# A three-layer graph network on one core: 28 of 98 receiver blocks summed from rows fetched by edge

## The chip, the core and the metric

The kernel runs on one core of one Trainium2 chip. The time is device microseconds from the start to the end of the launch, as the median of repeated runs. The core's engines work side by side, each through its own queue in order: TensorE (PE in the profile, with its weight loads shown as PEld), VectorE (DVE), ScalarE (ACT), GpSimd (POOL) and SyncE (SP, which here only issues transfers). Transfers run on 16 DMA engines.

## What is computed

There are 12,500 nodes with 64 values each, and 212,500 edges sorted by their receiving node (100,000 drawn pairs in both directions, and a loop for each node). Three mean-aggregating graph convolutions are followed by one network over edge attributes:

```
def _sage_conv(x, src, dst, Wl, Wr, b, n_nodes):
    msgs = x[src]
    summed = jax.ops.segment_sum(msgs, dst, num_segments=n_nodes)
    cnt = jax.ops.segment_sum(jnp.ones(src.shape[0], x.dtype), dst, num_segments=n_nodes)
    agg = summed / jnp.maximum(cnt, 1.0)[:, None]
    return agg @ Wl + x @ Wr + b
...
h = jnp.maximum(_layernorm(x, axis=-1), 0.0)
x = x + L0(h)        # three _sage_conv, relu after the first two
h = jnp.maximum(_layernorm(x, axis=-1), 0.0)
# L1: mean of the edge attributes by receiver, next to h, through 128->64->64->64
x = x + L1(h, edge_attr_64)
```

The segment sum is the work: for each receiver the rows of its senders are added, 17 edges per node on average.

## The kernel before

**Blocks and the matrix.** Nodes are cut into 98 blocks of 128. The kernel turns the edge list into a dense matrix of counts, senders by receivers, in 8-bit floats (a count in units of 1/64), and multiplies by it. One receiver block has 98 x 128 sender rows and 128 columns.

**Building it.** `index(j)` (L335) prepares four receiver blocks: one DVE pass over all tile heads (L340), three gathers on POOL (`ends`, `to`, `of`, all recorded on L330), some 30 small DVE instructions, and a transpose, which give for each edge its column number `col`, its low sender bits `lo` and a `weight`. `build` (L429) then takes a block in 26 steps, two at a time (`pair`, L434): per step DVE writes two one-hot tiles, `c` (128x245, L439) and `h` (128x128, L443), PE multiplies them (L447), and ACT writes two results as 16-bit words into the matrix tile `m` (L450). Two neighbouring blocks share one `m`, which SP stores to DRAM (`mat`, L466).

**Layer 0** (L482 to L509) walks over 49 pairs of blocks. While pair hp is multiplied, pair hp+1 is built. Node rows are held in SBUF as `parts`, each value split into three 16-bit parts. `dense` (L229) multiplies in two passes of 98 matmuls: the wide pass (L234) takes two parts of the rows as 128 weights, the narrow pass (L243) the third part as 64 weights, where even and odd sender blocks use the two halves of the array. In layer 0 the columns of one matmul are the 256 of a pair.

**Layers 1 and 2** (L547 to L699) read `mat` back through tiles `t` (L559, seven per group) and walk over 25 groups of four blocks, 512 columns per matmul (the last group has two blocks). `conv` (L251) adds the receiver's own rows (`turn`, L260) and multiplies by the weights (`mix`, L269 and L273); `relu_parts` (L217) writes the next layer's rows.

**Edges** are summed beside layer 2: for every block, `edge_sum` (L598) gathers 19 edges per partition (`raw`, L602) and their receivers (`eto`, L606), splits the values into three parts (ACT L612 and L614, POOL L613 and L615), writes 19 one-hots on DVE (`own`, L627) and adds with 19 matmuls (L631). `second` (L647) is the edge network.

**What sets the order.** PE's order is written by hand (`manual_schedule`): `woven` (L287) runs the dense matmuls and slips in the other pieces ("fills") at given fractions of a group. On the other engines the tile framework orders instructions and places the waits.

Of the kernel before, what the change touches and what calls it, by code (L numbers as in the profile page):

```python
# [9 lines left out]
F32 = mybir.dt.float32  # L10
I32 = mybir.dt.int32
BF16 = mybir.dt.bfloat16
U16 = mybir.dt.uint16
FP8 = mybir.dt.float8e3
# [23 lines left out]
EK = 19  # L38

# [21 lines left out]
def in_order(  # L61
# [23 lines left out]

    nc = tc.nc
# [4 lines left out]
    CW = HP * WD  # L91
    NG = -(-NB // 4)
    assert EP - sz.e >= EK and CW <= 256
# [23 lines left out]
    iota_l = const.tile([P, P], BF16, name="iota_l")  # L117
    pid = iota(const, "pid", 1, 1, per_partition=1)
# [5 lines left out]
    node0 = const.tile([P, NG], F32, name="node0")  # L124
    mask4 = const.tile([P, 4], F32, name="mask4")
# [60 lines left out]
    parts = [const.tile([P, NB, 3 * D], BF16, name=f"parts{i}") for i in range(2)]  # L186
    begins = const.tile([P, NG], F32, name="begins")
    cnt = const.tile([P, NG * 4], F32, name="cnt")
    inv = const.tile([P, NG * 4], F32, name="inv")
    twins = const.tile([P, NG, 4], F32, name="twins")  # L190
    nc.vector.memset(twins, 0.0)
    hts = [const.tile([D + 1, 4, P], F32, name=f"ht{i}") for i in range(2)]
    for t in hts:
        nc.gpsimd.memset(t[D : D + 1], 1.0)
    mat = [dram.tile([P, HP, 2 * P], U16, name=f"mat{i}") for i in range(HP)]

    ps_d = ctx.enter_context(tc.tile_pool(name="ps_dense", bufs=1, space=PSUM))
    ps_c = ctx.enter_context(tc.tile_pool(name="ps_conv", bufs=1, space=PSUM))
    conv_p = ctx.enter_context(tc.tile_pool(name="conv", bufs=2))
# [17 lines left out]
    def relu_parts(pool, o, to, bufs=None):  # L217

        n = o.shape[1]
        nc.scalar.activation(to[:, :, :D], o, AF.Relu)  # L220
        r = pool.tile([P, n, D], F32, name="rest", bufs=bufs)
        nc.vector.scalar_tensor_tensor(
            r, o, 0.0, to[:, :, :D], op0=ALU.max, op1=ALU.subtract
        )
        nc.scalar.copy(to[:, :, D : 2 * D], r)
        nc.vector.tensor_tensor(to[:, :, 2 * D :], r, to[:, :, D : 2 * D], op=ALU.subtract)


    def dense(rows, at, n):  # L229


        p1 = ps_d.tile([P, 4 * P], F32, name="p1")[:, :n]
        for i in range(NB):
            nc.tensor.matmul(  # L234
                p1, rows[:, i, : 2 * D], at(i), start=i == 0, stop=i == NB - 1
            )
            yield
        e1 = conv_p.tile([P, 4 * P], F32, name="e1", bufs=1)[:, :n]
        nc.scalar.copy(e1, p1)
        p2 = ps_d.tile([P, 4 * P], F32, name="p2")[:, :n]  # L240
        for i in range(NB):
            half = slice(D * (i % 2), D * (i % 2) + D)
            nc.tensor.matmul(  # L243
                p2[half], rows[:, i, 2 * D :], at(i), start=i < 2, stop=i >= NB - 2
            )
            yield
        agg = conv_p.tile([P, 4 * P], F32, name="agg")[:, :n]
        nc.vector.tensor_tensor(agg, e1, p2, op=ALU.add)  # L248
        return agg

    def conv(layer, rows, agg, j0, n):  # L251

        ht = hts[conv.turn]
        conv.turn ^= 1

        def turn():
            pt = ps_c.tile([D, 4, P], F32, name="pt")
            for k in range(n):
                for i in range(3):
                    nc.tensor.matmul(  # L260
                        pt[:, k, :], rows[:, j0 + k, D * i : D * i + D], identb,
                        start=i == 0, stop=i == 2,
                    )
            nc.scalar.copy(ht[:D, :n, :], pt[:, :n, :])

        def mix():
            po = ps_c.tile([P, 2, 4, D], F32, name="po")
            for k in range(n):
                nc.tensor.matmul(  # L269
                    po[:, 0, k, :], agg[:, k * P : (k + 1) * P], wl2[:, layer, :],  # L270
# [3 lines left out]
                    po[:, 1, k, :], ht[:, k, :], wr1[:, layer, :], start=True, stop=True  # L274
                )
            o = conv_p.tile([P, 4, D], F32, name="o")[:, :n, :]
            nc.vector.tensor_tensor(  # L277
                o, po[:, 0, :n, :], inv[:, j0 : j0 + n, None].to_broadcast([P, n, D]), op=ALU.mult
            )
            nc.vector.tensor_tensor(o, o, po[:, 1, :n, :], op=ALU.add)  # L280
            return o

        return turn, mix

    conv.turn = 0

    def woven(main, fills):  # L287

        fills = sorted(fills, key=lambda f: f[0])
        i = 0  # L290
        try:
            while True:
                while fills and fills[0][0] * 2 * NB <= i:
                    fills.pop(0)[1]()
                next(main)
                i += 1
        except StopIteration as e:
            for _, f in fills:
                f()
            return e.value  # L300


    with ExitStack() as s:
        idx = s.enter_context(tc.tile_pool(name="idx", bufs=2))
        ps_b = s.enter_context(tc.tile_pool(name="ps_build", bufs=3, space=PSUM))
        ps_i = s.enter_context(tc.tile_pool(name="ps_idx", bufs=1, space=PSUM))
        hot = s.enter_context(tc.tile_pool(name="hot", bufs=6))
        ln = s.enter_context(tc.tile_pool(name="ln", bufs=1))
        heads = s.enter_context(tc.tile_pool(name="heads", bufs=1)).tile([P, T], F32, name="heads")
        with tc.tile_pool(name="row", bufs=1) as r:  # L310
# [7 lines left out]
            for c in range(0, T, 512):  # L318
                n = min(512, T - c)
                ph = ps_b.tile([P, 512], F32, name="pb")  # L320
# [4 lines left out]
        mats = s.enter_context(tc.tile_pool(name="mats", bufs=3))  # L325
# [934 lines left out]
```

## Time and profile before

| what | value |
|---|---|
| median of 3 runs | 3513.1 us (3511.75 to 3513.64) |
| the profiled execution's own time | 3514.05 us |
| its span (first to last instruction) | 3512.3 us |
| granted TensorE clock | 0.992 |
| PE / DVE / ACT / POOL busy | 3350.0 / 2111.3 / 1196.0 / 750.7 us |
| HBM read and written | 389.97 and 160.56 MB |

A row of the profile's groups gives line, engine, operation, output<-inputs, the tile's shape, the count, then busy time in us and the mean duration of one in ns, then the idle time before the group and who ended it. Durations of neighbouring instructions on one engine can overlap, so their starts tell how fast they follow each other. PE matmuls are pipelined: the mean of one is a latency, and the busy time of a group divided by its count is nearer to its pace. A chain of waits lists start, length and what ran.

### The profile page before, as it was taken

How to read it: one execution, taken by the hardware profiler on the slowest of the kernel's cores; microseconds unless marked ns; L12 is line 12 of the kernel's file. 1: busy time of each engine (PE TensorE's matmuls, PEld its weight loads, DVE VectorE, ACT ScalarE, POOL GpSimd, SP SyncE). 2: the span in 40 equal slices, each digit the busy share in tenths (PEclk: the TensorE clock that was granted, in tenths of full speed). 3: DMA queues.
4: the chain of work that ended last, by engine and by line, in shares of the span. 5: the costliest groups of instructions: out<-in, count | busy, mean ns of one | idle time of the engine just before them, and what ended most of it. 6: DMA issues, size and time to landing. Idle time of an engine off the chain costs nothing.

```text
span 3512.3 us, 69396 instructions
## 1 busy us (share of the span) xinstructions
PE 3350.0 (95%) x26430; PEld 2019.0 (57%) x26430; DVE 2111.3 (60%) x9072; ACT 1196.0 (34%) x2101; POOL 750.7 (21%) x482
## 2 busy tenths in 40 slices
PE   1899999999999999999999999979999999999998
PEld 0566777777777777555454545544555555555555
DVE  8999999999999999300000000035556555555554
ACT  4555555555555555100000000022322322322232
POOL 1000000000000000000000000055555565555562
PEclk9999999999999999999999999989999999999999
DMA  2222222332223223645454545455455555555551
GB/s 45 115 116 118 115 116 115 137 129 115 115 120 146 115 111 134 233 155 220 155 212 165 202 176 191 170 218 181 176 182 211 204 206 181 176 183 211 204 193 53
DMA packets 168554, 555.12 MB, mean 158 GB/s; under 512 B 57793, under 2 KB 60386, under 8 KB 161938
## 3 DMA queue, kind: packets, MB, share of 16 engines
q1 hardware_dynamic: 133232, 478.53, 35.7%
q0 software_dynamic: 19648, 66.90, 5.6%
q10 hardware_dynamic: 15330, 5.16, 0.6%
q8 instruction: 208, 3.41, 0.4%
q14 instruction: 136, 1.11, 0.1%
HBM read 389.97 MB, written 160.56 MB: 157 GB/s over the span
## 4 chain that ended last, share of the span: by engine, by line
PE 84%; DVE 10%; issue 4%; DMA 1%; ACT 1%; POOL 0%; ACTq 0%; SPq 0%; DVEq 0%; POOLq 0%
PE p L234 40%; PE p L243 24%; PE pb L447 8%; PE pe L631 5%; DVE h L443 2%; DVE c L439 2%; PE po L273 2%; PE po L269 2%; PE pt L260 2%; DVE own L627 2%; PE ph L666 1%; PE mo L674 1%; DVE lower L340 0%; DVE junk L385 0%; PE mt L659 0%
## 5 line engine op out<-in xcount | busy, mean ns | idle before, releaser
L234 PEld LDWEIGHTS <-parts 128*128 128x128 bf16 x9702 | 937.2, 99 | 584.7 <-issue 46.2
L234 PE MATMUL p<-t,parts 128*128 128x512 fp8e3 (+1 forms) x4900 | 1106.7, 376 | 4.6 <-DMA t<-mat 4.6
L450 ACT CAST m<-pb 128x490 uint16<-128x490 f32 (+1 forms) x1274 | 717.4, 563 | 537.3 <-PE pb L447 534.4
L627 DVE TENSOR_SCALAR own<-iota_l,eplace 128x128 bf16<-128x128 bf16 x1862 | 548.2, 353 | 401.8 <-PE pe L631 401.4
L443 DVE TENSOR_SCALAR h<-iota_l,lo,weight 128x128 bf16<-128x128 bf16 x2548 | 779.8, 306 | 0.0
L439 DVE TENSOR_SCALAR c<-iota_c,col 128x245 bf16<-128x245 bf16 x2548 | 716.5, 281 | 10.9 <-PE pb L447 5.5
L243 PEld LDWEIGHTS <-parts 128*64 128x64 bf16 x9702 | 494.1, 109 | 387.8 <-issue 185.1
L234 PE MATMUL p<-m,parts 128*128 128x256 fp8e3 x4802 | 652.3, 273 | 0.6 <-ACT m L450 0.6
L243 PE MATMUL p<-t,parts 128*64 128x512 fp8e3 (+1 forms) x4900 | 584.4, 378 | 0.0
L447 PE MATMUL pb<-c,h 128*128 128x245 bf16 x2548 | 499.0, 274 | 52.4 <-DVE h L443 35.0
L248 DVE TENSOR_TENSOR agg<-e,p 128x256 f32<-128x256 f32 (+1 forms) x99 | 54.4, 549 | 603.2 <-PE p L243 600.3
L243 PE MATMUL p<-m,parts 128*64 128x256 fp8e3 x4802 | 409.3, 281 | 0.0
L602 POOL DMA_INDIRECT raw<-in_edge_dram,mine x98 | 93.7, 956 | 1124.9 <-DMA t<-mat 1098.6
L447 PEld LDWEIGHTS <-h 128*128 128x128 bf16 x2548 | 205.6, 98 | 204.0 <-DVE h L443 148.9
L613 POOL TENSOR_TENSOR erest<-raw,cut 128x1216 f32<-128x1216 f32 x98 | 244.2, 2492 | 202.2 <-issue 198.1
L631 PE MATMUL pe<-cut,own 128*128 128x192 bf16 x1862 | 227.0, 248 | 34.9 <-DVE own L627 17.5
L631 PEld LDWEIGHTS <-own 128*128 128x128 bf16 x1862 | 151.3, 98 | 166.4 <-issue 58.6
L615 POOL TENSOR_TENSOR cut<-erest,cut 128x1216 bf16<-128x1216 f32 x98 | 244.6, 2496 | 11.2 <-ACT cut L614 2.6
L612 ACT CAST cut<-raw 128x1216 bf16<-128x1216 f32 x98 | 118.1, 1205 | 275.6 <-PE pe L631 266.0
L277 DVE TENSOR_TENSOR o<-po,inv 128x128 f32<-128x128 f32 (+1 forms) x99 | 35.1, 354 | 271.8 <-PE po L273 271.6
L614 ACT CAST cut<-erest 128x1216 bf16<-128x1216 f32 x98 | 118.1, 1205 | 225.6 <-POOL erest L613 225.6
L330 POOL DMA_INDIRECT to<-in_dst_dram,at_i x25 | 23.6, 946 | 709.6 <-DVE at_i L358 595.8
(143 smaller groups left out, 1666.8 us busy)
## 6 DMA issues: line engine op xcount, KB each, us to landing
t<-mat SPq DMA_DIRECT2D x686, 448.0 KB, 6.1
mat<-m SPq DMA_DIRECT2D x49, 3136.0 KB, 10.0
xb<-in_x_dram SPq DMA_DIRECT2D x14, 224.0 KB, 2.7
xr<-in_x_dram ACTq DMA_DIRECT2D x24, 128.0 KB, 2.2
out_dram<-o SPq DMA_DIRECT2D x24, 128.0 KB, 2.0
raw<-in_edge_dram,mine POOLq DMA_INDIRECT x98, 5.4
eto<-in_dst_dram,mine POOLq DMA_INDIRECT x98, 3.7
here<-in_dst_dram ACTq DMA_DIRECT2D x4, 208.0 KB, 5.5
```

The source lines that it names most:

```text
L234: nc.tensor.matmul(p1, rows[:, i, : 2 * D], at(i), start=i == 0, stop=i == NB - 1)
L243: nc.tensor.matmul(p2[half], rows[:, i, 2 * D :], at(i), start=i < 2, stop=i >= NB - 2)
L439: nc.vector.tensor_scalar(c, iota_c, col[:, w : w + 1], None, op0=ALU.is_equal)
L443: nc.vector.tensor_scalar(h, iota_l, lo[:, w : w + 1], weight[:, w : w + 1], op0=ALU.is_equal, op1=ALU.mult,)
L447: nc.tensor.matmul(pb[:, i, :CW], h, c, start=True, stop=True)
L450: nc.scalar.copy(m[:, :, o : o + 2 * k].rearrange("p h (w d) -> p h w d", d=k), pb[:, :, :CW].rearrange("p w (h d) -> p h w d", d=WD)[:, : ...
L612: nc.scalar.copy(cut[:, :, :D], raw)
L613: nc.gpsimd.tensor_tensor(rest, raw, cut[:, :, :D], op=ALU.subtract)
L614: nc.scalar.copy(cut[:, :, D : 2 * D], rest)
L615: nc.gpsimd.tensor_tensor(cut[:, :, 2 * D :], rest, cut[:, :, D : 2 * D], op=ALU.subtract)
L627: nc.vector.tensor_scalar(o, iota_l, place[:, k : k + 1], 1.0 / UNIT, op0=ALU.is_equal, op1=ALU.mult,)
L631: nc.tensor.matmul(state["p"], o, cut[:, k, :], start=k == 0, stop=k == EK - 1)
```

## The change

Of the 98 receiver blocks, the first 28 (`GB`) no longer have a matrix. Their sums are made in every layer from the senders' rows themselves: rows are kept in DRAM (`h_d`, one copy per layer, 384 bytes a row), and 19 indirect transfers per block, each of 128 rows, bring them into a tile `got` in two halves (10 and 9). DVE writes the one-hots of a half in one instruction, and 19 matmuls of 192 columns add them up. The index lists `rows_of` and `place` for this are made in layer 0 from the edge list (`lists`).

The other 70 blocks keep the dense way, in 18 groups (17 of four blocks and one of two), in layer 0 too, where the matmuls now have 512 columns instead of 256. The group of two comes first in layer 0. Building writes the one-hots in batches of 6 or 8 steps, as two-tensor instructions on 16-bit values instead of instructions with a scalar per step; `h` takes a compare and a multiply. The one-hot buffers hold two batches, and PSUM's `pb` two tiles instead of three.

Rows of layer 0 and 1 leave through DRAM: layer 1 loads its rows again (`rows1`), layer 2 has them in SBUF (`rows2`) and in DRAM. The pieces between matmuls are placed by `Weave`: by the count of wide matmuls (`wide`), or at a place of the narrow pass (`narrow`). A fetched block comes every 61 wide matmuls. In layer 2 the edge sums lie at wide places only, ordered by need; their splitting subtractions moved from POOL to DVE, and their one-hots are batched. The checks at L512 to L544 moved into layer 1's loop.

```diff
+GB = 28
+H1 = 10
...
+    dense_groups = [(j, min(4, NB - j)) for j in range(GB, NB, 4)]
...
+    def onehot(pool, codes, k0, k1):
+        n = k1 - k0
+        t = pool.tile([P, H1, P], BF16, name="own")
+        nc.vector.tensor_tensor(
+            t[:, :n].rearrange("p k (c t) -> p k c t", t=2),
+            iota_l.rearrange("p (c t) -> p c t", t=2)[:, None].to_broadcast([P, n, D, 2]),
+            codes[:, k0:k1, None, :].to_broadcast([P, n, D, 2]),
+            op=ALU.is_equal,
+        )
+        return t
+
+    HALVES = ((0, H1), (H1, EK))
...
+        def fetch(self, i):
...
+            b, (k0, k1) = i // 2, HALVES[i % 2]
+            t = self.got.tile([P, H1, 3 * D], BF16, name="got")
+            for k in range(k0, k1):
+                nc.gpsimd.indirect_dma_start(
+                    out=t[:, k - k0, :], out_offset=None, in_=h_rows[self.l],
+                    in_offset=bass.IndirectOffsetOnAxis(ap=rows_of[:, b, k : k + 1], axis=0),
+                )
...
+        def use(self, b):
...
+            for h, (k0, k1) in enumerate(HALVES):
+                i = 2 * b + h
+                self.mark(i + 1)
+                o, t = self.owned.pop(i), self.fetched.pop(i)
+                for k in range(k0, k1):
+                    nc.tensor.matmul(
+                        self.pg[:, b % 2, :], o[:, k - k0, :], t[:, k - k0, :],
+                        start=k == 0, stop=k == EK - 1,
+                    )
+                self.fetch(i + self.bufs)
...
+            cuts = [(0, 8), (8, 14), (14, 20), (20, QW)]
...
+            def hots(i):
...
+                nc.vector.tensor_tensor(
+                    split(tc_), pairs(iota_c, CW), own(col, CW), op=ALU.is_equal
+                )
+                th = hot.tile([P, 8, P], BF16, name="h")
+                nc.vector.tensor_tensor(split(th), pairs(iota_l, P), own(lo, P), op=ALU.is_equal)
+                nc.vector.tensor_tensor(split(th), split(th), own(weight, P), op=ALU.mult)
...
-                    nc.vector.tensor_scalar(
-                        c, iota_c, col[:, w : w + 1], None, op0=ALU.is_equal
-                    )
-                    h = hot.tile([P, P], BF16, name="h")
-                    nc.vector.tensor_scalar(
-                        h, iota_l, lo[:, w : w + 1], weight[:, w : w + 1],
-                        op0=ALU.is_equal, op1=ALU.mult,
-                    )
...
+        slot = lambda b: 30 + 61 * (b + 1)
...
+            for b in range(GB):
+                w.wide(slot(b), lambda b=b: layer.use(b))
+            for t, g in enumerate(order):
+                if t + 1 < len(order):
+                    m_next, fills = matrix(order[t + 1])
+                    nw = 40 if len(fills) > 40 else len(fills)
+                    for i, f in enumerate(fills):
+                        if i < nw:
+                            w.wide(w.w + (i + 0.5) / nw * NB, f)
+                        else:
+                            w.narrow(w.w + 1, 6 + (i - nw) // 2 * 14, f)
...
+                layer.group(lambda i: view[:, : n // 2, i // 2, i % 2 :: 2], j0, n)
...
+        for a0 in range(0, NB, 14):
+            nc.scalar.dma_start(rows1[:, a0 : a0 + 14, :], h_d[1][:, a0 : a0 + 14, :])
...
+        def load(b):
...
+            raw = ed.tile([P, EK, D], F32, name="raw")
+            gather(raw.rearrange("p k d -> p (k d)"), edge, mine[:, b : b + 1])
+            if b < GB:
+                box[b] = raw, place[:, b]
+                return
...
+            nc.vector.tensor_tensor(rest, raw[:, k0:k1, :], c[:, :, :D], op=ALU.subtract)
...
-                nc.gpsimd.tensor_tensor(rest, raw, cut[:, :, :D], op=ALU.subtract)
```

## The prediction

> **What bounds the kernel now.** I read the busy shares, the slices, then the chain of waits stage by stage, then the pace of single operations. Busy shares and slices first (40 slices of 87.8 us each):
>
> ```profile
> PE 3350.0 (95%) x26430; PEld 2019.0 (57%) x26430; DVE 2111.3 (60%) x9072; ACT 1196.0 (34%) x2101; POOL 750.7 (21%) x482
> ...
> PE   1899999999999999999999999979999999999998
> DVE  8999999999999999300000000035556555555554
> POOL 1000000000000000000000000055555565555562
> ```
>
> PE is full nearly everywhere, DVE as well for the first 16 slices (layer 0), and POOL is idle until layer 2. The stages, in windows of 400 us (columns: window, length, then busy us and count of PE, PEld, DVE, ACT, POOL):
>
> ```profile
> 600.00:1000.00 400.00, 390.87 (x3885) 286.85 (x3884) 390.61 (x1900) 229.81 (x440) 21.87 (x23) 1.00 0.29 120
> 1800.00:2200.00 400.00, 400.00 (x2565) 201.44 (x2563) 27.90 (x59) 22.75 (x47) 0.00 (x0) 1.00 0.49 183
> 2800.00:3200.00 400.00, 394.26 (x2628) 206.08 (x2629) 229.74 (x809) 116.49 (x158) 229.54 (x133) 1.00 0.53 189
> ```
>
> Layer 0 keeps PE and DVE both at 98%, layers 1 and 2 are PE alone. The chain of waits gives the periods (start, length):
>
> ```profile
> 1438.75 5.47 PE p L243 x98
> ...
> 1488.26 4.42 PE p L234 x20
> 1494.41 14.68 PE p L234 x68
> 1509.09 10.70 PE p L243 x98
> 1522.84 4.42 PE p L234 x20
> ...
> 2805.70 2.59 PE p L234 x12
> ...
> 2853.80 2.59 PE p L234 x12
> ```
>
> A group of layer 1 takes 1522.84 - 1488.26 = 34.58 us: 98 wide matmuls at 0.216, 98 narrow at 0.109, 2.7 for turn and mix. A group of layer 2 takes 48.10. Layer 0's dense part runs from 104.0 (first L234 in the timeline) to 1444.2, 27.35 us for each of 49 pairs. The whole is 104 (start) + 1340 + 6 + 24.5 x 34.58 = 847, to 2297, + 24 (a gap before layer 2) + 24.5 x 48.10 = 1178, + some 13 = 3512. Pace of single operations, from the timelines of PE, DVE and POOL:
>
> ```profile
> 819.40 0.93 PE L234 MATMUL p<-m,parts 128*128 128x256 fp8e3 x7
> 820.16 0.37 PE L447 MATMUL pb<-c,h 128*128 128x245 bf16 x2
> 820.37 0.93 PE L234 MATMUL p<-m,parts 128*128 128x256 fp8e3 x7
> ...
> 714.54 0.30 DVE L443 TENSOR_SCALAR h<-iota_l,lo,weight 128x128 bf16<-128x128 bf16 x1
> 714.76 0.27 DVE L439 TENSOR_SCALAR c<-iota_c,col 128x245 bf16<-128x245 bf16 x1
> 714.95 0.30 DVE L443 TENSOR_SCALAR h<-iota_l,lo,weight 128x128 bf16<-128x128 bf16 x1
> ...
> 268.25 0.94 POOL L330 DMA_INDIRECT to<-in_dst_dram,at_i  x1 [2.83 <-DVE at_i L358]
> 269.50 0.94 POOL L330 DMA_INDIRECT of<-in_src_dram,at_i  x1 [0.30 <-issue]
> ```
>
> Read starts: two build matmuls cost PE 0.21 us in a wide pass (0.32 in a narrow one, from the same timeline), one step of `c` and `h` costs DVE 0.42, and a gather that waits for nothing follows the last after 1.25 (0.94 and 0.30 of issue).
>
> [...] In layer 0 gathers stayed at 0.94 us beside a DVE 98% busy, but with other instructions.
>
> **Dense work, all layers.** 24.5 groups become 17.5. In layers 1 and 2 that removes 7 x 34.58 = 242 us each. In layer 0, 49 pairs lose their 256-column matmuls (from the timeline 0.109 wide, 0.079 narrow, plus 1.3 for turn and mix: 19.7 us a pair, 965) and 17.5 groups of 34.58 = 605 come: 360 less.
>
> **Fetched blocks, each layer.** 28 x 19 = 532 matmuls of 192 columns. L631 has this shape; five follow each other in 0.41 us in wide passes: 532 x 0.082 = 44. Their seven convolutions need 7 x 3.0 (2.7 and a transpose) = 21. So 65 on PE.
>
> **POOL, the new resource.** 532 fetches a layer at 1.25 = 665 us. Bounds: 0.94 (no gap between, 500) and what long trains may cost, up to 2 us or more; a fetch moves 128 rows of 384 bytes, an `of` 128 of 512, so I take 1.25. In layer 1, PE needs per slot of 61 wide matmuls 21.5 (dense) + 1.6 + 0.75 = 23.9 us; POOL 19 x 1.25 = 23.75. They are level, hardly any cover is left.
>
> **Layer 1.** 605 + 65 = 670, + 15 for POOL being level. Start: rows through DRAM (agg, mix, relu, a store, then reload). 98 x 128 rows of 384 bytes are 4.8 MB, and the first group's seven `t` another 6.4 MB; `mat<-m` moved 3.2 MB in 10 us, so 35 us for what the wide pass eats in 21. I put 25 for the change of layer (6 before; bounds 10 and 45). Sum 710, before 853.
>
> **Layer 0, PE.** 17 full groups: 34.58 + 40 build pairs at 0.21 + 12 at 0.32 = 12.2, fetched 65/17.5 = 3.7, index matmuls 0.7: 51.2 us.
>
> **Layer 0, DVE.** [...] `c` costs 1.18 + 3 x 0.93, `h` twice 0.69 + 3 x 0.56: 8.7 us a block, less 12 overlaps of 0.08 (c lasts 0.28, the next starts after 0.20) = 7.7. Before it was 26 x 0.42 = 10.9. Four blocks 31; index work for 25 groups is now spread over 17.5, 1.42 x 7.5 (130 us beside one-hots in 600:1400 for 14 of them, less relu) = 10.7; one-hots, relu, sums, lists some 7. Together 49 us.
>
> **Layer 0, POOL.** 1.6 blocks x 23.75 = 38, index gathers 5.3, list gathers 4: 47.6, and each index waits in POOL's order for DVE between `ends` and `to` (2.8 us at best above), with fetches queued behind it, for which PE waits: 1.42 x 6 = 8.5, 56 in all. PE, DVE and POOL within 10%, in fixed orders and with only one batch of one-hots ahead, will wait on each other; I add 6.5 to PE's 51.2: 57.7 x 17 = 981. Bounds 51.2 (870) and 66. The first, small group must wait while four blocks are built (31 and 9): 40. Start 104 as now (DVE's row norms set it), end 8: 1133, before 1444.
>
> **Layer 2.** Dense 605 + 65; edges 98 x 19 x 0.082 = 153 (before part of them at 0.104 in narrow passes); the edge network 24.5 x 3.5 = 86 (two L666 pairs 2.0, L674 1.0, transposes 0.4): 909, against 1178. POOL per slot: 19 fetches, 3.5 `raw`, 2.5 `e_to` = 25 x 1.25 = 31.2, PE 32.3. POOL's order has fetches in trains of 19 with 3 to 5 `raw` between, and only two `raw` buffers: a train holds `raw` back for 23.75 us, while PE eats an edge block every 9.3. I add 45 (bounds 10 and 150). At the start 29 fetches precede the third block's `raw`, 36 us, while PE reaches it after some 14: 30 with transfers and splitting. Change of layer 20 (24 before). Sum 1004. POOL's old subtractions, 489 us, go to DVE, about 22 of 32 us busy per slot: hidden.
>
> **Sum.** 1133 + 710 + 1004 + 13 for the end = 2860; launch adds 1.75 (3514.05 - 3512.3), and the median of before lies 0.95 under its profiled run, so 2860.
>
> **The rivals.**
> 1. *The batched one-hots do not run at double rate.* Then a block costs (c 7.3, h 8.2, less 1) 14.5 us on DVE, a group 58 + 18 = 76, and layer 0 gets 17.5 x 18 = 315 longer: 3175. For it: no such instruction in the trace. [...] Chance 0.12.
> 2. *Gathers a little dearer in trains, 1.45 us* [...]. Layer 0: 62 a group, 1209; layer 1: 25 + 532 x 1.45 = 796; layer 2: 28.9 slots x 37 + 50 = 1120; 3138. [...] Against: 1.25 in every pair seen. Chance 0.12.
> 3. *POOL's queue becomes the whole bound, and the kernel is slower.* All three layers then last as long as POOL: 731 (start 144, index and list gathers 290, changes of layer 75, edge gathers 210, end 12) + 1596 x. It decides from x = (3512 - 731)/1596 = 1.74 us a fetch. Each fetch also waits for the landing of the eighth before it, so landings of 14 us would do it; `of` lands in 2.5, `raw` in 5.4. At 2.2 us: 4242. Chance 0.06.
> 4. *Everything hides.* Layer 0 at 51.2 (1017), layer 1 at 685, layer 2 at 940: 2655. Against: three engines level. Chance 0.09.
>
> The forecast has 0.60, and 0.01 is left for no change. 2680 to 3180 holds the forecast, most of rivals 1, 2 and half of 4: 0.8. Faster by over 0.2% (7 us, about what a measurement here can tell from no change) 0.93, within 0.01, slower 0.06.
>
> **What will show it.** In the new profile: starts of consecutive `got` gathers 1.25 us apart; `c` of 1476 elements near 930 ns (1.7 us means rival 1); a layer-1 group near 39 us per 98 wide matmuls with PE waiting little for `got`; in layer 0, some 58 us a group with waits of PE spread over `h`, `got`; a stall of tens of us at the start of layer 2 on `raw`. The prediction is wrong if PE's waits for `got` pass 150 us in layers 1 and 2 together, or if layer 0 ends before 1020 or after 1300.

## The result, and the profile after

The changed kernel took 4096.6 us (median of four runs, 4092.2 to 4111.6) against 3513.0 us before: a ratio of 1.167, 95% interval 1.164 to 1.170. It is slower, where 2860 us were forecast. To read the numbers below: a later run of the same kernel, on another occasion, took 3544 us, while the kernel before took 3511 to 3516 us on all of them, so the loss has one part that is always there and one part, some 550 us, that comes and goes.

The profiled execution of the record took 4111.6 us. Its page, busy times and slices of 103 us:

```profile
PE 2942.0 (72%) x18603; PEld 1642.6 (40%) x18603; DVE 1651.8 (40%) x3691; ACT 994.9 (24%) x1837; POOL 1936.9 (47%) x1910
...
PE   1467776677667895877877787767687777667767
...
POOL 2444553445444534445545544455545555455451
PEclk9978888778788997878878888878888778887887
```

PE was 95% busy before and is 72% busy now (73, 78 and 72% in the three layers), and no other engine is full: POOL, which was feared, is busy 47%. The granted clock fell with it (0.833, 0.992 before). The groups of instructions (same columns as before):

```profile
L345 PE MATMUL p<-t,rows 128*64 128x512 fp8e3 x3332 | 562.2, 432 | 181.4 <-issue 174.3
...
L424 PE MATMUL pg<-got,own 128*128 128x192 bf16 x1596 | 150.2, 250 | 2.3 <-issue 1.3 <-DMA got<-h_d,rows_of 1.0
...
L649 DVE TENSOR_TENSOR c<-iota_c,col 128x1476 bf16<-128x1476 bf16 x210 | 194.3, 925 | 205.0 <-remote 95.2 <-PE pb L667 86.6 <-PE pi L567 7.5
```

What the prediction priced is there as priced: `c` of 1476 elements takes 925 ns, and PE waits 1.0 us in all for fetched rows (`got`). But L345, plain dense matmuls with all their data on chip, sat idle 174 us with nothing to wait for ("issue"). The windows of the three layers, from first to last dense matmul (columns as before: window, length, busy us and count of PE, PEld, DVE, ACT, POOL, then clock, DMA share, GB/s):

```profile
143.00:1550.00 1407.00, 1027.03 (x6679) 579.22 (x6678) 816.05 (x1994) 524.05 (x980) 637.67 (x616) 0.84 0.30 105
1578.00:2636.00 1058.00, 830.33 (x4754) 418.10 (x4752) 98.45 (x198) 47.56 (x96) 507.58 (x524) 0.83 0.41 134
2643.00:4079.00 1436.00, 1033.10 (x6973) 614.99 (x6970) 622.65 (x1134) 371.36 (x657) 727.04 (x696) 0.82 0.46 143
```

Layer 1 has nearly no work on DVE and ACT and lasts 1058 us where 685 were expected. What PE does there in "issue", from its timeline (start, length, what ran and how often; in brackets the idle time ahead of it):

```profile
1909.19 1.46 PE L334 MATMUL p<-t,rows 128*128 128x512 fp8e3 x6
...
1913.30 0.38 PE L334 MATMUL p<-t,rows 128*128 128x512 fp8e3 x1 [0.62 <-issue]
1914.73 1.01 PE L334 MATMUL p<-t,rows 128*128 128x512 fp8e3 x2 [1.05 <-issue]
```

A dense matmul follows the last after 0.22 us when PE is at its pace (61 of them in 13.33 us, from 1893.59 on); here they come in ones and twos. The starts of PE's single instructions in the trace lie 0.70 or 1.40 us apart in these stretches (329 such distances in layer 1, 284 us; none in the layers 1 and 2 of the kernel before); below they are called gaps. In layer 1 all of them lie in the later part of a train of fetches, from the seventh fetch in a row on, or within 5 us of its last one; the stretch shown lies in a train from 1893 to 1917 us. POOL nearly keeps its pace: in the whole kernel 1147 of the distances between fetches are 1.25 us and 44 are 1.40.

Not only PE's starts are late. The other engines learn of PE's work late as well. This is from PE's and ACT's timelines just after that train, the last turning matmuls of a group and the copy that needs them:

```profile
1936.41 0.41 PE L365 MATMUL pt<-identb,rows 128*64 128x128 bf16 x2 [0.45 <-issue]
...
1947.82 0.58 ACT L369 COPY ht<-pt 64x512 f32<-64x512 f32 x1 [16.48 <-remote]
```

By the trace the matmuls end at 1936.8, and ACT, idle, starts 11.0 us later. "remote" names a release that fits the end of no instruction; it stands at `c` above too. PE reports finished work by semaphore updates, which the trace holds with their times. In the three layers 621 of 3092 of them come over 0.15 us after the recorded end of the last PE instruction that makes one, by up to 19.6 us. In the later run without gaps there are 10 of 3361, by up to 0.6 us (the median is 0.014), and no engine has a wait named "remote". The updates of DVE and ACT are no later on record than there (4 and 2 late ones in the whole kernel, against 2 and 2). In layer 0, where PE has few gaps (31 distances, 25 us), DVE stood 190 us and ACT 227 us ahead of instructions that were released in this way.

### The profile page after: what moved, and what is told of

Its sections match the earlier page's. It is cut to its first block, busy times and chain, and to the rows that moved or that the text cites. A ratio compares the mean times of both kernels' runs of the same rounds, so it can differ in the third digit from the quotient of the medians.

```text
span 4109.9 us, 46926 instructions
## 1 busy us (share of the span) xinstructions
PE 2942.0 (72%) x18603; PEld 1642.6 (40%) x18603; DVE 1651.8 (40%) x3691; ACT 994.9 (24%) x1837; POOL 1936.9 (47%) x1910
## 3 DMA queue, kind: packets, MB, share of 16 engines
q1 hardware_dynamic: 108608, 353.28, 23.5%
## 5 line engine op out<-in xcount | busy, mean ns | idle before, releaser
L398 POOL DMA_INDIRECT got<-h_d,rows_of x1596 | 1632.0, 1023 | 1378.2 <-PE pg L424 839.4
L334 PE MATMUL p<-t,rows 128*128 128x512 fp8e3 (+1 forms) x3528 | 872.8, 394 | 79.8 <-issue 58.1
L334 PEld LDWEIGHTS <-rows 128*128 128x128 bf16 x5292 | 538.7, 104 | 544.9 <-issue 201.0
L345 PE MATMUL p<-t,rows 128*64 128x512 fp8e3 (+1 forms) x3528 | 575.9, 423 | 181.4 <-issue 174.3
L670 ACT CAST m<-pb 128x490 uint16<-128x490 f32 (+1 forms) x910 | 498.8, 563 | 818.5 <-PE pb L667 453.6
L345 PEld LDWEIGHTS <-rows 128*64 128x64 bf16 x5292 | 345.1, 118 | 591.7 <-issue 444.9
L334 PE MATMUL p<-m,rows 128*128 128x512 fp8e3 (+1 forms) x1764 | 538.5, 401 | 3.1 <-issue 2.2
L649 DVE TENSOR_TENSOR c<-iota_c,col 128x1476 bf16<-128x1476 bf16 (+1 forms) x280 | 276.9, 989 | 279.1 <-remote 123.2
L300 DVE TENSOR_TENSOR own<-iota_l,place 128x1280 bf16<-128x1280 bf16 (+1 forms) x224 | 175.8, 786 | 370.1 <-remote 219.7
L345 PE MATMUL p<-m,rows 128*64 128x512 fp8e3 (+1 forms) x1764 | 249.4, 404 | 6.5 <-issue 6.0
```

Of the source, the lines that this page charges most:

```text
L300: nc.vector.tensor_tensor(t[:, :n].rearrange("p k (c t) -> p k c t", t=2), iota_l.rearrange("p (c t) -> p c t", t=2)[:, None].to_broadcast ...
L334: nc.tensor.matmul(p1, rows[:, i, : 2 * D], at(i), start=i == 0, stop=i == NB - 1)
L345: nc.tensor.matmul(p2[h], rows[:, i, 2 * D :], at(i), start=i < 2, stop=i >= NB - 2)
L398: nc.gpsimd.indirect_dma_start(out=t[:, k - k0, :], out_offset=None, in_=h_rows[self.l], in_offset=bass.IndirectOffsetOnAxis(ap=rows_of[:, ...
L649: nc.vector.tensor_tensor(split(tc_), pairs(iota_c, CW), own(col, CW), op=ALU.is_equal)
L670: nc.scalar.copy(m[:, block // 2, :, o : o + 2 * k].rearrange("p h (w d) -> p h w d", d=k), pb[:, :, : HP * WD].rearrange("p w (h d) -> p ...
```

## The experiments

All times are one profiled run each unless a count is given; layers are measured as in the windows above. "Gaps" are distances of 0.70 or 1.40 us between PE instructions, counted in the trace.

### Without the fetches

```diff
+            self.zero = self.pool.tile([P, H1, 3 * D], BF16, name="zero", bufs=1)
+            nc.vector.memset(self.zero, 0.0)
...
-            t = self.got.tile([P, H1, 3 * D], BF16, name="got")
...
-            self.fetched[i] = t
+            self.fetched[i] = self.zero
```

> The changed kernel with all 1596 fetches left out: the matmuls of the 28 blocks read one tile of zeros, so their sums are missing from the output. Theory A (trains of fetches are what costs: they starve PE while they run and hold index and raw gathers back in POOL's queue): PE's gaps of 0.70 us vanish, the granted clock returns to over 0.97, layer 1 takes about 700 us in place of 1150, and the whole is 2650 to 2850 us. Theory B (the hand-written order, with one batch of one-hots ahead and edge work at wide places only, makes PE wait whatever POOL does): the whole stays above 3600 us and the clock below 0.9.

It took 2856.8 us at a clock of 0.966: theory A, though a little outside its 2850 us and its 0.97. The windows of its layers:

```profile
119.00:1162.00 1043.00, 943.51 (x6679) 552.86 (x6679) 807.89 (x1996) 524.11 (x980) 118.76 (x113) 0.96 0.29 118
1192.00:1875.00 683.00, 681.79 (x4751) 390.15 (x4753) 98.52 (x198) 47.49 (x96) 0.00 (x0) 0.99 0.45 168
1882.00:2824.00 942.00, 922.41 (x6971) 579.65 (x6971) 619.96 (x1136) 371.08 (x659) 177.82 (x164) 0.98 0.55 191
```

PE is full in layers 1 and 2, layer 1 has no gap at all, and PE, DVE and ACT execute what they execute on record. So the whole loss of 1240 us comes with the 1596 fetches, 0.78 us each on average, though nearly nothing waits for their rows.

### A train that nobody waits for

```diff
-            self.fetched[i] = t
+            self.fetched[i] = self.zero if self.l == 1 else t
```

> The changed kernel in which, in layer 1 alone, the matmuls of the 28 blocks read a tile of zeros (their layer 1 sums are left out), while the fetches are still made, with no reader, so that they run as one train from the start of layer 1. Theory A1 (a running train slows PE by itself, although nobody waits for what it brings): from some 10 us into the layer until the train ends, about 665 us later, PE issues with gaps of 0.70 us at a low clock, and then runs at 34.6 us a group; layer 1 takes 900 us or more. Theory A2 (what costs is the coupling, PE waiting for fetched rows and POOL for PE): layer 1 takes about 700 us and PE has no gaps.

4436.8 us, layer 1 1368 us: theory A1. Two windows of it, during the train and after it, and PE's timeline in the train:

```profile
1600.00:2290.00 690.00, 124.47 (x253) 30.78 (x252) 4.23 (x8) 1.99 (x4) 529.42 (x511) 0.51 0.19 50
2320.00:2950.00 630.00, 627.79 (x4351) 358.73 (x4351) 94.37 (x190) 44.23 (x90) 0.00 (x0) 0.98 0.44 161
```

```profile
1629.36 0.58 PE L337 MATMUL p<-t,rows 128*128 128x512 fp8e3 x1 [2.22 <-issue]
1632.16 0.58 PE L337 MATMUL p<-t,rows 128*128 128x512 fp8e3 x1 [2.22 <-issue]
```

While POOL fetches, PE starts a matmul every 2.80 us, a matmul or weight load every 1.40, with one stop of 74 us (from 2100.5 on), over 690 us; DMA engines are busy 19% of the time, and apart from that stop PE has nothing to wait for. When the train is over, the same work runs at full pace.

The stop shows where the delay lies. PE waits there for DVE's sum `agg` of the group before, which starts at 2174.1, though PE's last narrow matmul of that group ended by the trace at 2086.4. ACT's copy of the wide pass's sums starts at 1866.0, the last wide matmul having ended at 1778.4. In both cases PE's semaphore update comes 87.6 us after the recorded end, the time of about 63 instructions at 1.40 us. So, read from this trace, PE's work is reported as finished at one instruction per 1.40 us, and its recorded starts run only a limited way ahead of that: 102 instructions go at full pace before the first gap, and the work after the stop catches up again (485 instructions in 680 us, stop included, are one per 1.40).

The clock of 0.51 in the first window goes with a PE that does little: a matmul lasts 0.58 us here, 0.38 at full clock (381 ns in the mean of the wide pass before, at a granted 0.992), and between two matmuls PE idles 2.22 us while the clock stays at half (0.50 to 0.52 in each 100 us from 1700 to 2300). It is a consequence, not the cause: on record each of the 23 stretches of gaps in layer 1 begins while the clock is 1.00.

### Pauses in the trains, and few fetches

```diff
+                if self.l == 1 and (k % 5 == 4 or k == EK - 1):
+                    for _ in range(3):
+                        nc.gpsimd.memset(self.nap, 0.0)
```

> The changed kernel with a pause in layer 1: after every fifth fetch of a block POOL clears a scratch tile three times, about 3 us. Only trains of at most five are left in layer 1, and POOL needs 28 x (19 x 1.25 + 4 x 3) = 1000 us there. Theory A3 (the slowing begins only where a train goes on for 7 fetches or more): the gaps of 0.70 us vanish in layer 1, which is then bound by POOL and takes about 1010 us, over 100 less than in the changed kernel, though POOL does more. Theory A4 (every fetch costs PE something, in trains or not): layer 1 takes 1150 us or more.

4170.6 us, layer 1 1101 us with 353 gaps. This doesn't decide: the framework, which orders POOL's instructions, drew the pauses together, and the trace still shows trains of 19 (2033 to 2055 us) between long rows of clears.

```diff
-GB = 28
+GB = 4
...
-                pos = min((i + 0.3) / NB * span, due)
+                pos = at_w[i]
```

> The changed kernel with 4 fetched blocks in place of 28 (94 dense), and in layer 2 the edge pieces spaced so that each block is summed before it is due. With 4 x 19 fetches a layer there is little of the trains. If the fetches are what costs, the batched one-hots and the 512-column matmuls of layer 0 are left as gains: layer 0 24 groups of about 50 us, layer 1 24 x 34.6, layer 2 24 x 46, with start and end 3300 us, below both kernels. If the order by places or the batched one-hots cost time themselves, it is slower than 3513 us.

3458.8 us beside 3513.1, one run each: faster than both, by 1.5% over the kernel before, on an occasion with gaps, but 159 us above the 3300 expected. Its 76 fetches a layer left 49 gaps, 43 us, in layer 1. Layer 0 lasted 1235 us for 23.5 dense groups and four fetched blocks, against 1340 for 24.5 groups before. Per dense group that is 52.6 us against 54.7, so about half of the 105 us is one group less, and the rest is what the batched one-hots and the 512-column matmuls bring, less what the fetches cost there. Layers 1 and 2 gained nothing (872 and 1179 us).

### Pace, rows, kind: and an occasion without gaps

Three further runs, again with a train in layer 1 that nobody reads: 190 fetches with POOL in a fixed order and pauses between, 532 fetches of 64 rows, and 532 plain transfers from POOL's queue.

```diff
+                if self.l == 1:
+                    nc.gpsimd.memset(self.nap, 0.0)
+                    nc.gpsimd.memset(self.nap, 0.0)
```

> In layer 1 the matmuls of the 28 blocks read a tile of zeros (their layer 1 sums are left out); 190 fetches with no reader are still made there, and POOL, in a fixed order, clears a scratch tile twice after each (0.95 us each), so that one fetch starts every 3.2 us for about 610 us. Without fetches layer 1 lasted 683 us; with a train it lost 1.29 us for each fetch. Theory S (PE's front end is held up only while a fetch is being made, and PE's own queue covers a short stop): PE keeps its pace, no gaps of 0.70 us, layer 1 at 683 to 720 us. Theory T (each fetch takes a fixed toll from PE, however spaced): 190 x 1.29 = 245 us more, layer 1 at 900 us or more.

```diff
+                h = P // 2 if self.l == 1 else P
...
-                    out=t[:, k - k0, :], out_offset=None, in_=h_rows[self.l],
+                    out=t[:h, k - k0, :], out_offset=None, in_=h_rows[self.l],
```

> As the run with a free train in layer 1 (sums of the 28 blocks there left out, 532 fetches with no reader), but every fetch brings 64 rows in place of 128. If the toll goes with the rows (descriptors), PE loses about half as much, some 340 us over 683, and layer 1 takes about 1030 us. If it goes with the instruction, layer 1 takes about 1370 us as with 128 rows.

```diff
+                if self.l == 1:
+                    nc.gpsimd.dma_start(t[:, k - k0, :], h_d[1][:, (7 * i + k) % NB, :])
+                    continue
```

> As the run with a free train in layer 1 (sums of the 28 blocks there left out), but each of the 532 fetches is a plain transfer of 128 rows of 384 bytes from POOL's queue, at addresses fixed in the program. If the toll comes from the software-made transfers of POOL as such, PE again issues one instruction per 1.4 us while they run and layer 1 takes 1000 us or more. If it comes from the indexed gather alone, layer 1 takes about 690 us.

All three had 682 or 683 us in layer 1 and no gap there. That looked like an answer to three questions at once, and was none: their layers 0 and 2, where nothing had been changed, had also lost their gaps (layer 2: 1, 2 and 2 of them in place of 138). The occasion was another one. So the unchanged kernel and the free train were run together with the next two:

> The changed kernel as it is, once more, beside the three that follow. In the runs with 190 paced fetches, half fetches and plain transfers, not only layer 1 but the untouched layers 0 and 2 were free of PE's 0.70 us gaps (layer 0 1280 us in place of 1407 to 1436, layer 2 1390 in place of 1436 to 1453), and those runs were on another chip. Theory U (the toll belongs to some chips): here the kernel takes either about 4100 us with such gaps or about 3900 to 3950 without them, and the free train behaves alike. Theory V (the toll depends on the kernel, say on what ran in layer 1): 4100 us with gaps whatever the chip.

> The free train of 532 fetches with no reader in layer 1 once more (sums of the 28 blocks there left out). Theory U: layer 1 at about 1370 us if the changed kernel beside it shows gaps of 0.70 us, about 683 us if it shows none. Theory V: 1370 us in either case.

> The 190 paced fetches with no reader in layer 1 once more (sums of the 28 blocks there left out). If the changed kernel beside it shows the gaps: theory S (a fetch every 3.2 us leaves PE time to fill its queue) 683 to 720 us in layer 1, theory T (a fixed toll for each fetch) 900 us or more. If it shows none: 683 us, and nothing is told.

> The 532 fetches of 64 rows with no reader in layer 1 once more (sums of the 28 blocks there left out). If the changed kernel beside it shows the gaps: about 1030 us in layer 1 if the toll goes with the rows, about 1370 us if with the instruction, 683 us if there is a rate of rows below which nothing is lost. If it shows none: 683 us, and nothing is told.

The unchanged kernel took 3544.4 us beside 3511.6 (0.9% slower), with 1 gap in layer 1, and the free train of 532 fetches left layer 1 at 686 us. Theory V, that the kernel alone decides, falls. Theory U's wording, that it belongs to some chips, fell later: the chip of the first four runs was met again for the last three, and showed no gaps. Paced fetches were run twice more for this and half fetches once (e14, e17 and e18, with their expectations below); each time no run beside them had gaps, layer 1 was 682 or 683 us, and whether pace or rows matter stays untold. That PE has a queue which a pause lets it fill, as theory S supposes, was not shown by any run.

The run of the unchanged kernel is what shows the part that is always there. Its layers:

```profile
123.00:1404.00 1281.00, 980.45 (x6681) 567.48 (x6679) 814.65 (x1996) 525.03 (x980) 654.67 (x628) 0.87 0.33 116
1433.00:2120.00 687.00, 683.38 (x4754) 390.79 (x4752) 98.55 (x198) 47.49 (x96) 503.43 (x524) 0.98 0.61 206
2127.00:3511.00 1384.00, 981.64 (x6965) 605.97 (x6967) 623.44 (x1134) 370.02 (x657) 732.48 (x696) 0.83 0.46 149
```

Layer 1 is as without fetches, layer 0 is 238 us and layer 2 442 us longer. No engine is full, so it is a matter of waits. The waits of PE and of DVE (engine, line, whom it waited for, total us, times, longest), first layer 0, then layer 2:

```profile
PE pb L667 <- DVE h L654: 229.7, 52, 23.3
...
PE pe L889 <- DVE cut L881: 113.9, 6, 32.8
```

```profile
DVE pos L527 <- DMA to<-in_dst_dram,at_i: 135.3, 15, 19.4
DVE place L617 <- DMA l_to<-in_dst_dram,mine: 105.9, 22, 16.0
...
DVE e_rest L879 <- ACT cut L878: 428.6, 24, 30.9
```

PE waits for DVE, which is 64% busy in layer 0 and 45% in layer 2, and for ACT, which is less so; they in turn stand still for a gather: DVE in layer 0 at the first reader of `to` and of `l_to`, in layer 2 behind ACT's first split of `raw` (`cut`), which itself waited 502 us for `raw` to land. Why `raw` is late shows in one stretch of the timelines of POOL and ACT, the end of a train of fetches:

```profile
2599.87 1.10 POOL L398 DMA_INDIRECT got<-h_d,rows_of  x1 [0.30 <-issue]
2601.28 0.95 POOL L492 DMA_INDIRECT raw<-in_edge_dram,mine  x1 [0.30 <-issue]
...
2607.95 0.72 ACT L878 CAST cut<-raw 128x640 bf16<-128x640 f32 x1 [14.52 <-DMA raw<-in_edge_dram,mine]
```

POOL issues `raw` after the train, at 2601.3, and ACT, idle since 2593.4, starts on it at 2608.0. While ACT and DVE stand at one instruction, the one-hots, sums and network pieces behind it in their queues stand too, and PE runs out of what they make.

### POOL's order by hand

```diff
+            for k in range(k0, k1):
+                if at is None:
+                    piece(k)
+                else:
+                    self.weave.wide(at + STEP * (k - k0), lambda k=k: piece(k))
...
-        with tc.manual_schedule(engines={PE}):
+        with tc.manual_schedule(engines={PE, POOL}):
...
-            raw = ed.tile([P, EK, D], F32, name="raw")
+            raw = ed.tile([P, EK, D], F32, name="raw", bufs=3)
...
-                    load(blocks[i + 2])
+                    load(blocks[i + 3])
```

> The changed kernel with POOL's order written by hand: the fetches of a block are issued one by one, three wide matmuls apart, so that index, list and raw gathers come between them; in layer 2 three raw buffers in place of two, each loaded one block earlier, and the first three raw loads stand before the first fetches. The same 1596 fetches are made. Theory Q (outside layer 1 the loss is DVE and ACT standing still for a gather that waits in POOL's queue behind a train): the loss against the run without fetches, 238 us in layer 0 and 442 us in layer 2 where no 0.70 us gaps are seen, falls to less than half: layer 0 at 1050 to 1160 us, layer 2 at 950 to 1150, the whole at 2880 to 3150 us. Rival (POOL's sheer load of 1.25 us a fetch bounds these layers): they stay above 1250 and 1300 us, and the whole above 3400. With the 0.70 us gaps of the first chip, add about 550 us to each.

> As the run with POOL's order by hand, but with 12 fetched blocks in place of 28 (86 dense). PE has 16 x (3 x 8.6 - 3 x 2.3 + 12) = 490 us more to do, POOL half the fetches. Without the 0.70 us gaps: about 3250 us. With them, the toll should shrink with the fetches (684 of 1596), to some 240 us or less: 3500 us at most.

> The 190 paced fetches with no reader in layer 1 a third time (sums of the 28 blocks there left out). Where the runs beside it show the 0.70 us gaps: 683 to 720 us in layer 1 if a pause of 1.9 us after each fetch lets PE fill its queue, 900 us or more if each fetch takes a fixed toll. Where they show none: 683 us, and nothing is told.

No gaps on this occasion. With 28 fetched blocks 3388.0 us beside 3512.8, 3.6% faster than the kernel before; with 12, 3473.1, where some 3250 were expected. Layers 0 and 2 with 28 blocks, and DVE's waits in each:

```profile
118.00:1391.00 1273.00, 973.35 (x6679) 559.40 (x6678) 812.95 (x1996) 524.58 (x980) 663.44 (x635) 0.88 0.34 117
...
2108.00:3356.00 1248.00, 1005.58 (x6974) 621.36 (x6973) 623.63 (x1135) 371.18 (x657) 749.15 (x695) 0.88 0.51 165
```

```profile
DVE junk L521 <- DMA ends<-in_dst_dram,tile_i: 208.2, 22, 20.1
...
DVE e_at L875 <- DMA e_to<-in_dst_dram,mine: 391.1, 62, 30.8
```

Layer 2 won 136 of the 442 us, layer 0 only 8: neither theory's numbers are met. The order and the number of `raw` buffers changed together, so what of the 136 us belongs to which isn't told. POOL's load is not the bound (52 and 60% busy; at 1.25 us an instruction, pauses included, an estimate gives 62 and 70%). DVE's wait at `e_rest` went from 428.6 to 5.8 us, but the wait moved rather than went: in layer 0 DVE now stands at `ends`, in layer 2 at `e_at`, the first reader of `e_to`. POOL waited 269 us in layer 0 for PE to give back a half of `got`, with `ends` behind the waiting fetch.

### Readers put later

```diff
             ends = idx.tile([P, P], I32, name="ends")
             gather(ends, tiles_d, tile_i[:, :1])
+            yield
...
             gather(of, src, at_i[:, :1])
-
+            yield
...
-                w.wide(w.w + 8, lambda t=t: begin(order[t + 2]))
+                w.wide(w.w + 8, lambda t=t: begin_late(order[t + 2]))
```

> The run with POOL's order by hand, and now DVE reads what a gather brings later in its own order: index work is cut into three parts, 24 wide matmuls apart, with the gather at the end of one part and its first reader at the start of the next; the lists' readers and the receivers of an edge block (e_at) stand likewise later. In the run before, DVE stood still 208 us at the first reader of ends in layer 0 and 391 us at e_at in layer 2. Theory Q2 (the loss left in layers 0 and 2 is DVE, in order, standing at the reader of a gather still on its way): layer 0 from 1273 to 1150 us or less, layer 2 from 1247 to 1100 or less, the whole at 3050 to 3150 us where there are no 0.70 us gaps. Rival (PE's waits come from POOL's fetches or from the one batch of one-hots ahead): both layers within 50 us of what they were, 3290 to 3390.

> The run with POOL's order by hand and late readers once more; the first time it met a chip with the 0.70 us gaps (4093 us). Theory Q2 where the runs beside it show no such gaps in layer 1: layer 0 at 1150 us or less (1273 with POOL's order alone), layer 2 at 1100 or less (1247), the whole at 3050 to 3150 us. Rival: both within 50 us of what they were, 3290 to 3390. With the gaps: about 4090 again.

> The 190 paced fetches with no reader in layer 1 (sums of the 28 blocks there left out), a last time. Where layer 2 of the same run shows the 0.70 us gaps: 683 to 720 us in layer 1 if a pause of 1.9 us after each fetch lets PE fill its queue, 900 us or more if each fetch takes a fixed toll. Where it shows none: 683 us, and nothing is told.

> The 532 fetches of 64 rows with no reader in layer 1 (sums of the 28 blocks there left out), a last time. Where layer 2 of the same run shows the 0.70 us gaps: about 1030 us in layer 1 if the toll goes with the rows, about 1370 us if with the instruction, 683 us if there is a rate of rows below which nothing is lost. Where it shows none: 683 us, and nothing is told.

The first time the gaps were back (355 in layer 1, 1057 us; four runs 4065 to 4107 us, 1.165 of before, interval 1.159 to 1.171). The second time, without gaps, 3430.6 us: layer 0 1313, layer 2 1238. Both layers are within 50 us of what they were, as the rival had it, though the whole is above its 3390. But the run didn't do what it was made for, so it decides nothing. In layer 0 DVE stood 157.6 us at `ends` and 103.9 at `to`, where it had been 208.2 and 15.6, and POOL stood 408 us for a half of `got`. DVE's wait in layer 2:

```profile
DVE e_at L923 <- DMA e_to<-in_dst_dram,mine: 390.6, 61, 29.5
```

It is the wait of the run before to half a microsecond: on DVE the framework sets the order, and `e_at` stands among the same neighbours as before, however late the program names it. Whether layers 0 and 2 come back to 1043 and 942 us when DVE's order too is by hand wasn't tried.

## Why the prediction was wrong

The stages of the prediction against three profiled runs (us; the rows for layers include the change of layer ahead of them):

| stage | predicted | no fetches | gap-free occasion | on record |
|---|---|---|---|---|
| to the first dense matmul | 104 | 119 | 123 | 143 |
| layer 0 | 1029 | 1043 | 1281 | 1407 |
| layer 1 | 710 | 713 | 716 | 1086 |
| layer 2 | 1004 | 949 | 1391 | 1443 |
| end | 13 | 31 | 32 | 31 |
| span | 2860 | 2855 | 3543 | 4110 |

- **Right, by its own steps.** The dense work, the cost of 192-column matmuls, the batched one-hots (1182 and 925 ns for `c`, 1.18 and 0.93 us forecast; 683 and 552 for the compare of `h`, 0.69 and 0.56) and the fetches' pace of 1.25 us. The double rate itself, against 32-bit instructions of the kind, was the author's estimate, which the profile before, without such an instruction, doesn't show. The runs do: a 16-bit `own` of 1152 elements took 749 ns, a 32-bit `e_rest` of 576, also with two tensor inputs, 754. At the pace of the 32-bit L207 before (417 ns for 256 elements, 621 for 448) an estimate gives 1.7 us for `c` of 1476, and some 7.4 and 8.2 us for `c` and `h` of a block, close to what rival 1 reckons with. Rival 1 (no double rate) and rival 2 (dearer fetches in trains: they average 1.02 us and mostly follow each other after 1.25) are out. That the sum of 2860 us lies 3 us from the kernel without fetches is luck: it contains 15 + 6.5 x 17 + 45 + 30 us for waits among the engines, and stage by stage it misses that run by -15, -14, -3, +55 and -18 us, which cancel.
- **Mis-sized: "a train holds `raw` back".** Layer 2's term was 45 us, bounds 10 and 150, and 30 at the start. The waits are there, the size is 442 us against the run without fetches (idle PE 402 - 20 = 382, longer busy time at a lower clock 60). The step took only PE's own wait for `raw`: a train of 23.75 us against an edge block every 9.3. It left out that ACT and DVE wait in order (DVE 428.6 us at `e_rest` alone), so that pieces that need no `raw` wait as well, and that POOL's next `raw` then waits for them in turn.
- **Mis-sized: "they will wait on each other; I add 6.5".** In layer 0 that was 6.5 us a group on top of PE's 51.2. Against the run without fetches 238 us were lost, 14 us for each of 17 groups more. The step counted POOL waiting for DVE (1.42 x 6), with fetches queued behind; the costly direction was the other one, DVE standing up to 19 us at a reader of `to` or `l_to`, which sat in POOL's queue behind fetches, with the one-hots for PE behind that reader. These two rows rest on the waits in the traces and on the run without fetches, where DVE stood only 20 and 32 us at these two readers. No run kept the fetches and took all these waits away, so that they are the whole of the 238 and 442 us is not shown.
- **Missing: what fetches do to PE.** "Fetched blocks, each layer" priced PE at 65 us and no more, and "PE waits for `got`" was the only way the forecast knew for a fetch to reach PE. On the record occasion the same kernel was longer than on the gap-free one by 126 us in layer 0, 371 in layer 1 and 52 in layer 2. In layer 1 that is mostly PE's own slow pace (284 us lie in its gaps). In layer 0 its gaps are 25 us, and the traces point to DVE and ACT, which learn late of what PE has done and then keep it waiting; how much of the 126 us that makes was not separated. Nothing in the profile before could show it: there at most four gathers ever followed each other.
- **Rival 3** named the right sign for another reason. POOL was not the bound (47% busy), and landings cost little: the fetches take eight semaphores in turn (111 to 118 in the trace), so that each waits for the landing of the eighth before it, but POOL stood only 16.5 us in all ahead of fetches for such a landing, and PE 1.0 us for `got`. The stop line of 150 us on such waits was never near, while the one on layer 0 (end after 1300) was crossed at 1404 and 1550.

On the gap-free occasion the change is still slower, by 0.9% (one run), so the sign of the forecast was wrong even without the gaps, by the two mis-sized terms.

The best version measured where there were gaps is the one with few fetches, at 3458.8 us. With all fetches and POOL's order by hand 3388.0 us were reached where there were no gaps, and the kindred version with late readers took 4093 us where there were.

## What stays open

What the gaps depend on. They showed in the four record runs, in the first four experiments (those of them that fetch) and in the four runs of one later version; of kernels run one after the other, either all that fetch showed them or none did; the same chip showed them once and not another time. That fetches are needed is shown by the one run without them on such an occasion, and by gaps that lie only in trains and just after them. The late semaphore updates mark the same runs: by 12.5 to 87.6 us in each run with gaps, by at most 0.7 in every run without, the one without fetches among them. By what way a fetch delays the report of PE's work is not shown. Two candidates find no support in the traces. Packets of the fetches took longer on record (196 ns in the median, 156 on the gap-free occasion; those of `t` 140 on both), but they took 196 in layer 0 of the run with POOL's order by hand as well, and there were no gaps. The transfers of the profile's first queue of kind `instruction` (q8, 147 of 16 KB each) took 0.98 and 0.97 us in the slow 690 us, no longer than elsewhere (1.0), and PE's pace doesn't change at them. Every run on record comes with a traced span and clock, so whether the gaps come without tracing is not known. Pace, rows and kind of transfer could be tried only where there were no gaps to lose.

## What to carry to other kernels

Before work is moved to a gather queue, list what already goes through that queue and who stands, in order, at the first reader of each of its results: the trains of 19 fetches left POOL with time to spare (53% busy in layer 2 of the gap-free run), and still a single `raw` issued after one kept ACT idle for 14.5 us, and with it everything behind that reader. An order written out for one engine doesn't bind the others: a piece that must be late on DVE or spread on POOL has to be ordered there. When an engine waits for nothing that the profile names, compare the recorded end of an instruction with the start of what it releases: here PE's reports came up to 87.6 us after the recorded ends, and on record ACT stood idle 16.48 us ahead of a copy and started it 11.0 us after its matmuls had ended by the trace. And a reading taken on one occasion should have a control run beside it, or three experiments can agree on nothing.

## What the runs showed of the hardware that was not expected

- On an occasion with gaps PE started one instruction per 1.40 us in a train of indexed fetches (485 in 680 us), after going on at its pace for 13 us (102 instructions), and its semaphore updates came 87.6 us after the recorded ends. Late in the train POOL's own fetches, 1.09 us and 0.30 between two, came 1.40 us apart too, and PE kept that pace for 22 us after the last fetch. The same train left PE at its full pace on another occasion (686 us for the layer, 1368 with gaps).
- Batched bf16 one-hots with two tensor inputs: 552, 925 and 1182 ns for 768, 1476 and 1968 elements. An estimate from the first and the last is 0.525 ns for each further element and some 149 ns that don't go with them. The 32-bit L207 before (417 ns for 256 elements, 621 for 448) gives 1.06 and some 145 in the same way: twice the time for an element, and nearly the same fixed part.
- A fetch of 64 rows occupied POOL 0.90 us and one of 128 rows 0.94 (medians where there were no gaps), so most of a fetch's time there doesn't go with its rows.
